# Vision stack of RWKV layers and a graph convolution: loads of x placed in mid-step, the first conv product ahead of the sums, and a variance subtracted by TensorE

## The chip, the cores and the metric

The kernel runs on one core of a Trainium2 chip. The time is that of the device in microseconds (us) for one launch, the median of several runs; less is better. A core has a matrix engine (TensorE, PE), three engines for elementwise work (VectorE or DVE, ScalarE or ACT, GpSimd or POOL), and an engine that only issues transfers (SyncE, SP). Each has its own instruction stream, and semaphores tie the streams together.

## The reference

The input x has 16 images of 192 channels and 56 x 56 pixels in float32. Three layers of one kind follow each other, then one of another kind. Cut to what matters:

```python
for l in 0, 1, 2:
    xs = tokens(group_norm(x, 32 groups))             # [16, 3136, 192]
    k, v, r = xs @ Wk.T, xs @ Wv.T, xs @ Wr.T
    h = sigmoid(r) * 0.5 * (wkv(k, v) + flip(wkv(flip(k), flip(v))))
    h = (h - mean(h)) * rsqrt(var(h) + 1e-5)          # over the 192 channels
    x = x + image((h * ln_g + ln_b) @ Wo.T)
g = group_norm(x)
m = max over the four rolls of g by 2 rows or columns, minus g, and 0
x = x + gelu(batch_norm(conv_1x1(concat(g, m))))
```

`wkv` is a recurrence over the 3136 tokens: a numerator p and a denominator q decay by a factor of each channel at every token and take in exp(k) * v and exp(k); the result is a quotient with a bonus for the present token. The other direction runs the same from the end. The reference carries a running maximum to keep the exponentials in range.

## The kernel before

**Tiles.** The images are taken in pairs. A pair's 192 channels twice are 384 rows, kept as three blocks of 128 partitions: a chunk of 448 tokens (`L`, one seventh of an image, `NL` = 7) is a tile of 128 x 3 x 448. Such tiles live in 33 slots. `Slot(...)` (L502) takes the oldest name of the list `free`, and `give` puts it back at the end; both happen while the program is written, so which tile comes into which slot is fixed by the order of the code, and an instruction that writes into a slot waits for those that still read the tile before. The banks of PSUM are handed out in the same manner (L513 to L523): seven banks, each of which holds 128 x 512.

**Runs and steps.** A pair in a layer is a run. A run of an RWKV layer first goes forward over its seven chunks (units A: products k and v, exp, forward scans, forward quotient), then backward (units B: product r for the gate, backward scans and quotient, mean of both directions, gate, layer norm, output product, new x with its statistics for the next group norm). A run of the conv layer has units C. Two streams of pairs are shifted against each other, so that a step joins a backward chunk of one run with a forward chunk of another. The program has 249 steps. A step can also carry z: statistics of the input of a pair which starts later; for these the chunk of x is loaded for this alone (units Z).

**Order.** Every engine runs in the order in which the code issues its instructions. Each kind of step has an order written by hand, over small functions that issue for one engine each: `both_a` (85 steps, B with A), `both_a_first` (17, B with A where an earlier chunk's layer norm has not begun), `both_c` (42 steps in seven phases of six, B with C), and `forward_a`, `forward_c`, `backward_alone` for the rest. The main loop (L1686 on) passes the units of the present and of the next step (`nback`, `nfront`). In `both_a` the gate product of the next B stands at the start and the keys of the next A in the middle of the step. `of_stage` says which chunk's layer norm stands at which stage; it's spread over two steps or more.

**Transfers of x.** `load_ahead(unit)` (L830) loads the chunk of x for a unit, if it's not there, into a new slot; a unit C also gets a ring of neighbours. All loads and stores of x are issued by SP, in order: before the change the main loop loads the Z chunks of the present step and the backward chunk of two steps ahead, then the step function loads `nback` and `nfront` (mostly only the latter is new), and `store` writes finished output of the conv layer. Later in a step `b_x` stores the new x (L1089).

**Layer norm of a chunk.** `b_squares` (ScalarE) squares the gated h. `b_sums` (L1037 on; TensorE) sums h and its square over channels: rows 0 to 63 (`LO`) of the bank `st` hold the means, 32 equal rows for each image, and rows 64 to 127 (`HI`) the mean squares. `b_rs1` (L1050, ScalarE) squares the mean, `b_rs2` (L1054, VectorE) subtracts it from the mean square, and `b_rs3` (L1059, L1060, ScalarE) takes exp(-0.5 ln(var + eps)). `b_spread` (L1066, TensorE) spreads this over the channels with ones in `pick`; `b_scale` (L1071, VectorE) multiplies, `b_out` does the output product, and `b_x` (L1084, VectorE) adds it to x. The mean itself is taken out by the output weights, which are folded with a centring matrix at the start.

**Other lines that the prediction names.** `scan` (L870): VectorE's scans, three per direction and operand, over 449 elements each. `bonus` (L885): VectorE's `q` or `p` plus bonus. `save` (L881): copies the scan's last state to the next tile. `a_ekv` (L935): exp(k) * v. `a_y` (L977): GpSimd's product of numerator and inverse denominator in the forward direction; it gives back the denominator's slot at once. `b_mix` (L1026 to L1028): GpSimd's three products and sums for the mean of both directions and the gate. `project` (L593 to L602): a product with a folded matrix of 192 x 192 for both images, in float32.

Of the kernel before, what the change touches and what calls it, by code (L numbers as in the profile page):

```python
# [473 lines left out]
def fast_path(ctx: ExitStack, tc: tile.TileContext, flag, x, wproj, wfold, wcfold, wconst, wgroup, sums, picks, vecs, out):  # L474
# [562 lines left out]
    def b_sums(run, c):  # L1037
        h, sq = run.h[c].t, run.ek.pop(c)
        st = run.ps["st"] = bank("st")
        parts = ((h, 0), (h, 1), (sq.t, 0), (sq.t, 1))  # L1040
        for n, (t, i) in enumerate(parts):
            PE.matmul(st[32 * n : 32 * n + 32, :L], ones[:, 0, :], t[:, 2 * i, :], start=True, stop=False)
        for n, (t, i) in enumerate(parts):
            PE.matmul(st[32 * n : 32 * n + 32, :L], ones[:, 1 + i, :], t[:, 1, :], start=False, stop=True)
        sq.give()

    def b_rs1(run, c):
        rs, st = row.tile([P, L], F32, tag="rs", name=name("rs")), run.ps["st"]
        run.rs[c] = rs
        S.activation(rs[HI, :], st[LO, :L], AF.Square)  # L1050

    def b_rs2(run, c):
        rs, st = run.rs[c], run.ps["st"]
        V.tensor_sub(rs[HI, :], st[HI, :L], rs[HI, :])  # L1054
        release(st)

    def b_rs3(run, c):
        rs = run.rs[c]
        S.activation(rs[HI, :], rs[HI, :], AF.Ln, bias=eps4[HI, :])  # L1059
        S.activation(rs[HI, :], rs[HI, :], AF.Exp, scale=-0.5)  # L1060

    def b_spread(run, c):
# [252 lines left out]
        for _ in range(min(most, len(z))):  # L1315
            z_stats(*z.pop(0))

    def both_a(b, a, nback, nfront, z):

        den = lambda: a[0].den[a[1]]  # L1320
        l = of_stage(0.5)
        load_ahead(nback)
        load_ahead(nfront)
        store()
        if nback is not None:
            b_gate(*nback[1:])
            b_exp(*nback[1:])
        count(z)
        b_q(*b)
        if l:  # L1330
            b_rs2(*l)
            b_rs3(*l)
        b_sigmoid(*b)
        a_values(*a)
        if l:
            b_spread(*l)
        b_p(*b)
        b_den(*b)
        for js in (AC, slice(1, 2)):
            ln(b[0].ek[b[1]], js)  # L1340
            exp_minus(b[0].ek[b[1]], js)
        b_num(*b)
        b_mix(*b)
        if l:
            b_scale(*l)
            b_out(*l)
            late[l] = 2
        a_ekv(*a)
        sum_up()
        keys(nfront)  # L1350
        a_q(*a)
        if l:
            add(l)
        b_squares(*b, (0,))
        a_save(*a)
        count(z)
        exp_keys(nfront, (0, 2))
        b_squares(*b, (2,))
        exp_keys(nfront, (1,))
        b_squares(*b, (1,))  # L1360
        b_sums(*b)
        a_p(*a)
        gap()
        a_den(*a)
        b_rs1(*b)
        late[b] = 0.5
        invert(den())
        gap()
        a_num(*a)
        a_y(*a)  # L1370
        gap()

    def both_a_first(b, a, nback, nfront):

        den = lambda: a[0].den[a[1]]
        l = of_stage(0)
        load_ahead(nback)
        load_ahead(nfront)
        store()
        a_values(*a)  # L1380
        b_squares(*l, (0, 2))
# [4 lines left out]
        invert(b[0].ek[b[1]])  # L1386
        b_num(*b)
        b_mix(*b)
        a_ekv(*a)
        b_squares(*l, (1,))  # L1390
        if nback is not None:
# [22 lines left out]
        exp_minus(den())  # L1414
        a_y(*a)

    def both_c(b, a, nback, nfront):

        l0, l1, l2 = of_stage(0), of_stage(1), of_stage(2)
        load_ahead(nback)  # L1420
        load_ahead(nfront)
        store()
        b_q(*b)
        b_p(*b)
        if l0:
            squares_and_sums(l0)
        b_den(*b)
# [7 lines left out]
        if l1:  # L1435
            spread_and_scale(l1)
        gap()
        if nback is not None:
            b_gate(*nback[1:])
            b_exp(*nback[1:])  # L1440
        else:
            keys(nfront)
            exp_keys(nfront)
        c_product(*a, 0)
        c_rows(*a)
        c_columns(*a)
        c_product(*a, 1)
        gap()
        if l0:
            b_rs2(*l0)  # L1450
            b_rs3(*l0)
            late[l0] = 1
        gap()
        b_num(*b)
        b_sigmoid(*b)
# [223 lines left out]
    with tc.manual_schedule(engines={PE.engine, V.engine, S.engine, G.engine, nc.sync.engine}):  # L1679
# [6 lines left out]
        for i, (b, f, z) in enumerate(steps):  # L1686
# [3 lines left out]
            if i == 0:  # L1690
                keys(f)
                exp_keys(f)
            for run, c, _ in z:
                load_ahead(("Z", run, c))
            if i + 2 < len(steps):
                load_ahead(steps[i + 2][0])

            nkeys = nfront if nfront is not None and nfront[0] == "A" else None
            if f and not b and nkeys is None and nfront is not None and i + 2 < len(steps):
# [3 lines left out]
            if f and nback is None and nfront is not None:  # L1703
                near = [u for _, u, _ in steps[i + 1 : i + 4] if u is not None and u[0] == "A"]
                if len(near) > 1 and near[1][1] is near[0][1]:
                    load_ahead(near[1])
            if b and f and f[0] == "A":
                if of_stage(0) is None:
                    both_a(b[1:], f[1:], nback, nfront, z)
                else:  # L1710
                    both_a_first(b[1:], f[1:], nback, nfront)
            elif b and f:
                both_c(b[1:], f[1:], nback, nfront)
            elif f and f[0] == "A":
                forward_a(f[1:], nback, nfront, nkeys, z)
            elif f:
# [60 lines left out]
def _lay_out(inputs):  # L1777
# [10 lines left out]
    for q in layer:  # L1788
# [8 lines left out]
    sums = np.zeros((P, 3, 32), np.float32)  # L1797
    sums[:, 0, :] = sums[0:64, 1, :] = sums[64:P, 2, :] = 1.0 / C

    picks = np.zeros((P, 3, P), np.float32)  # L1800
    picks[64, 0, :] = picks[64, 1, 0:64] = picks[96, 1, 64:P] = picks[96, 2, :] = 1.0
    return {"x": x, "wproj": wproj, "wconv": wconv, "wconst": wconst, "ones": ones, "vecs": vecs,
            "wfold": wfold, "wcfold": wcfold, "wgroup": _pack_rows(group), "sums": sums, "picks": picks}

# [18 lines left out]
```

## Time and profile before

| what | value |
|---|---|
| median of 3 runs | 5291.94 us (5285.85 to 5298.13) |
| the profiled execution's own time | 5294.96 us |
| its span | 5293.2 us |
| mean granted TensorE clock in it | 0.917 of full |
| VectorE busy | 4893.1 us (92%) |
| TensorE busy | 4618.0 us (87%) |
| ScalarE busy | 3705.1 us (70%) |
| GpSimd busy | 2883.5 us (54%) |
| mean HBM traffic | 90 GB/s |
| the subtraction L1054 | 168 times 628 ns, 105.5 us |

The span is the time from the first to the last instruction on the core; busy times are those in which an engine executes. An engine's busy share is an average over steps with different limits, so the waits of each engine and the timeline of single steps have to be read beside it. A row of instructions has its line, engine, operation, output and input with the number of partitions and elements, the count, then the total and mean duration, and the idle time ahead of it with what ended most of it. A row of waits reads: engine, line and tile that waited, what released it, us in total, number of waits, the longest. In a timeline the columns are the start, the duration, and the instruction.

### The profile page before, as it was taken

The page shows a single profiled execution, that of the slowest core. Times are in us where ns is not written, and L with a number is a line of the kernel's source. Part 1 is how long each engine was busy: PE and PEld are TensorE (multiplying, and loading weights), DVE is VectorE, ACT ScalarE, POOL GpSimd, SP SyncE. Part 2 cuts the span into 40 slices and gives each one's busy share as a digit, 9 for nine tenths or more (in the row PEclk, how much of TensorE's full clock was granted, in tenths as well). Part 3 has the DMA queues.
Part 4 walks back from the last instruction along what each step waited for, and adds up shares of the span by engine and source line. Part 5 has one row for each costly group of instructions (what it writes and reads, how often), then busy time and mean ns, then how long its engine had stood idle before and what let it go on. Part 6 is the DMA issues. An engine that isn't in the chain of part 4 may idle for free. (4 is left out here: it accounts for less than half of the span.)

```text
span 5293.2 us, 51222 instructions
## 1 busy us (share of the span) xinstructions
PE 4618.0 (87%) x15206; PEld 1484.1 (28%) x15206; DVE 4893.1 (92%) x6456; ACT 3705.1 (70%) x7163; POOL 2883.5 (54%) x2234
## 2 busy tenths in 40 slices
PE   7888888889798888888979888888897988898897
PEld 3222222223232222222323222222232322222222
DVE  6999899899999998999999999889999999999996
ACT  6777777776666777777666677777756667777672
POOL 1665555554545555555454555555545455566562
PEclk9999989989899899889989988888998999999898
DMA  5222222233332222223333222222333322222233
GB/s 151 68 81 86 83 81 91 84 107 112 92 103 82 74 87 98 71 88 124 93 98 106 74 83 87 86 83 87 122 92 103 92 73 76 78 81 79 69 107 113
DMA packets 314272, 482.43 MB, mean 91 GB/s; under 512 B 66432, under 2 KB 306688, under 8 KB 313984
## 3 DMA queue, kind: packets, MB, share of 16 engines
q1 hardware_dynamic: 312832, 477.59, 28.2%
q8 instruction: 123, 2.02, 0.2%
q10 hardware_dynamic: 1152, 1.48, 0.1%
q14 instruction: 165, 1.35, 0.1%
HBM read 324.83 MB, written 154.14 MB: 90 GB/s over the span
## 5 line engine op out<-in xcount | busy, mean ns | idle before, releaser
L870 DVE TENSOR_TENSOR_SCAN q<-fdecays,ek 128x449 f32<-128x449 f32 (+1 forms) x1008 | 1024.7, 1071 | 60.8 <-POOL p L977 50.5
L870 DVE TENSOR_TENSOR_SCAN p<-fdecays,ekv 128x449 f32<-128x449 f32 (+1 forms) x1008 | 1024.1, 1071 | 44.9 <-POOL p L977 42.4
L977 POOL TENSOR_TENSOR p<-p,q 128x1344 f32<-128x1344 f32 x168 | 512.3, 3050 | 856.6 <-ACT q L973 437.6
L1026 POOL TENSOR_TENSOR ekv<-ekv,ek 128x448 f32<-128x448 f32 x504 | 624.0, 1238 | 588.1 <-ACT ek L973 211.1
L1028 POOL TENSOR_TENSOR p<-p,sg 128x448 f32<-128x448 f32 x504 | 609.3, 1209 | 78.5 <-ACT ek L879 31.9
L1027 POOL TENSOR_TENSOR p<-p,ekv 128x448 f32<-128x448 f32 x504 | 601.7, 1194 | 39.5
L881 POOL COPY ekv<-p 128x3 f32<-128x3 f32 x265 | 231.3, 873 | 678.6 <-DVE p L870 660.0
L915 ACT ACTIVATE ek<-k,k 128x448 f32<-128x448 f32 x504 | 295.2, 632 | 316.0 <-PE k L596 274.8
L593 PE MATMUL ops<-p,fwo 128*128 128x448 f32 x336 | 235.6, 792 | 268.3 <-DVE p L1071 268.1
L1035 ACT ACTIVATE ek<-p 128x448 f32<-128x448 f32 x504 | 282.7, 572 | 217.3 <-POOL p L1028 216.5
L1066 PE MATMUL rsb<-rs,fpicks 32*128 32x448 f32 (+1 forms) x1008 | 353.6, 618 | 90.2 <-ACT rs L1060 90.2
L730 ACT ACTIVATE fjunk<-x 128x448 f32<-128x448 f32 x672 | 387.6, 577 | 41.5 <-DVE x L1084 14.6
L1084 DVE SCALAR_TENSOR_TENSOR x<-ops,fwob,x 128x448 f32<-128x448 f32 x504 | 317.9, 673 | 73.5 <-PE ops L596 39.9
L885 DVE SCALAR_TENSOR_TENSOR ek<-ek,fcc,q 128x896 f32<-128x896 f32 x336 | 374.9, 1156 | 0.1
L729 ACT ACTIVATE fjunk<-x 128x448 f32<-128x448 f32 x600 | 342.5, 571 | 11.4
L885 DVE SCALAR_TENSOR_TENSOR q<-ek,fcc,q 128x896 f32<-128x896 f32 x336 | 345.7, 1070 | 2.2 <-ACT ek L879 1.6
L970 ACT ACTIVATE q<-q 128x1344 f32<-128x1344 f32 x168 | 222.8, 1326 | 162.0 <-DVE q L885 134.0
L991 ACT ACTIVATE sg<-r,r 128x448 f32<-128x448 f32 x504 | 312.9, 627 | 20.1 <-PE r L596 14.4
L935 DVE SCALAR_TENSOR_TENSOR ekv<-v,v,ek 128x448 f32<-128x448 f32 x504 | 313.7, 676 | 12.5 <-PE v L602 7.1
L1071 DVE TENSOR_TENSOR p<-p,rsb 128x448 f32<-128x448 f32 x504 | 281.7, 614 | 46.3 <-PE rsb L1066 46.0
L885 DVE SCALAR_TENSOR_TENSOR ekv<-ekv,fcc,p 128x896 f32<-128x896 f32 x336 | 322.4, 1001 | 1.2
L885 DVE SCALAR_TENSOR_TENSOR p<-ekv,fcc,p 128x896 f32<-128x896 f32 x336 | 294.7, 918 | 4.3 <-POOL ekv L881 2.1
(235 smaller groups left out, 11544.5 us busy)
## 6 DMA issues: line engine op xcount, KB each, us to landing
x<-xd SPq DMA_DIRECT2D x240, 672.0 KB, 5.8
xd<-x SPq DMA_DIRECT2D x168, 672.0 KB, 4.1
x<-in_x_dram SPq DMA_DIRECT2D x320, 224.0 KB, 4.2
x<-in_x_dram SPq DMA_DIRECT2D x320, 112.0 KB, 4.0
out_dram<-ml SPq DMA_DIRECT2D x112, 224.0 KB, 2.3
m<-xd SPq DMA_DIRECT2D x112, 168.0 KB, 5.3
wkv<-in_wfold_dram SPq DMA_DIRECT2D x24, 640.0 KB, 5.3
out_dram<-ml SPq DMA_DIRECT2D x112, 112.0 KB, 2.3
```

The source lines that it names most:

```text
L729: S.activation(junk, xt[:, j, :], AF.Identity, accum_out=stats[:, 0, j, c : c + 1])
L730: S.activation(junk, xt[:, j, :], AF.Square, accum_out=stats[:, 1, j, c : c + 1])
L870: V.tensor_tensor_scan(out, dec[:, column(j)].to_broadcast([P, L if first else L + 1]), e, 0.0, ALU.mult, ALU.add)
L885: by_channel(lambda js, i: V.scalar_tensor_tensor(dst.t[:, js, :], e.t[:, js, :], cc[:, i : i + 1], state.t[:, js, :], ALU.mult, ALU.add))
L935: V.scalar_tensor_tensor(e.t[:, j, :], ps[j][:, 0:L], b[:, j, :], run.ek[c].t[:, j, :], ALU.add, ALU.mult)
L977: G.tensor_mul(run.h[c].t, run.h[c].t, den.t)
L991: S.activation(sg.t[:, j, :], ps[j][:, 0:L], AF.Exp, bias=b[:, j, :], scale=-1.0, accum_out=run.chk[:, at : at + 1])
L1026: G.tensor_mul(y.t[:, j, :], y.t[:, j, :], den.t[:, j, :])
L1027: G.tensor_add(h.t[:, j, :], h.t[:, j, :], y.t[:, j, :])
L1028: G.tensor_mul(h.t[:, j, :], h.t[:, j, :], sg.t[:, j, :])
L1066: PE.matmul(ps[j][:, :L], pick[rows, j, :], rs[rows, :], start=True, stop=True)
L1084: V.scalar_tensor_tensor(xj, ps[j][:, 0:L], wob[:, column(j)], xj, ALU.add, ALU.add, accum_out=run.new[:, 0, j, c : c + 1] if c == 0 else ...
```

## The change

It has three parts. The layer norm's variance: the square of the mean is written to the lower half of its tile, TensorE multiplies it by a negative unit matrix (64 x 64, new in the constant `picks`) and adds it onto the mean square in the bank `st`, and Ln reads the bank. The loads: `nfront`, the Z chunks (now those of the next step) and the backward chunk of two steps ahead go into a list, `loads`, which `both_a` and `both_a_first` load after `b_mix`, and `both_c` after its first `gap` and the conv's `store`; other steps load it at their start, as before. `both_a_first` also takes the slot for the next `ekv` ahead of the loads. The conv step: where no layer norm is at stage 1 and a backward unit follows (`first`), the gate product of the next B, its exp and the first half of the conv product come ahead of the squares and sums. In all of `both_c` the subtraction and what follows it move ahead of `c_columns` and the second conv product.

```diff
--- before.py
+++ after.py
@@ -1041,22 +1041,22 @@
         for n, (t, i) in enumerate(parts):
             PE.matmul(st[32 * n : 32 * n + 32, :L], ones[:, 0, :], t[:, 2 * i, :], start=True, stop=False)
         for n, (t, i) in enumerate(parts):
-            PE.matmul(st[32 * n : 32 * n + 32, :L], ones[:, 1 + i, :], t[:, 1, :], start=False, stop=True)
+            PE.matmul(st[32 * n : 32 * n + 32, :L], ones[:, 1 + i, :], t[:, 1, :], start=False, stop=n < 2)
         sq.give()
 
     def b_rs1(run, c):
         rs, st = row.tile([P, L], F32, tag="rs", name=name("rs")), run.ps["st"]
         run.rs[c] = rs
-        S.activation(rs[HI, :], st[LO, :L], AF.Square)
+        S.activation(rs[LO, :], st[LO, :L], AF.Square)
 
     def b_rs2(run, c):
+        PE.matmul(run.ps["st"][HI, :L], pick[LO, 0, 0:64], run.rs[c][LO, :], start=False, stop=True)
+
+    def b_rs3(run, c):
         rs, st = run.rs[c], run.ps["st"]
-        V.tensor_sub(rs[HI, :], st[HI, :L], rs[HI, :])
+        S.activation(rs[HI, :], st[HI, :L], AF.Ln, bias=eps4[HI, :])
         release(st)
-
-    def b_rs3(run, c):
-        rs = run.rs[c]
-        S.activation(rs[HI, :], rs[HI, :], AF.Ln, bias=eps4[HI, :])
         S.activation(rs[HI, :], rs[HI, :], AF.Exp, scale=-0.5)
 
     def b_spread(run, c):
@@ -1315,12 +1315,11 @@
         for _ in range(min(most, len(z))):
             z_stats(*z.pop(0))
 
-    def both_a(b, a, nback, nfront, z):
+    def both_a(b, a, nback, nfront, z, loads):
 
         den = lambda: a[0].den[a[1]]
         l = of_stage(0.5)
         load_ahead(nback)
-        load_ahead(nfront)
         store()
         if nback is not None:
             b_gate(*nback[1:])
@@ -1341,6 +1340,8 @@
             exp_minus(b[0].ek[b[1]], js)
         b_num(*b)
         b_mix(*b)
+        for u in loads:
+            load_ahead(u)
         if l:
             b_scale(*l)
             b_out(*l)
@@ -1370,12 +1371,11 @@
         a_y(*a)
         gap()
 
-    def both_a_first(b, a, nback, nfront):
+    def both_a_first(b, a, nback, nfront, loads):
 
         den = lambda: a[0].den[a[1]]
         l = of_stage(0)
         load_ahead(nback)
-        load_ahead(nfront)
         store()
         a_values(*a)
         b_squares(*l, (0, 2))
@@ -1386,6 +1386,9 @@
         invert(b[0].ek[b[1]])
         b_num(*b)
         b_mix(*b)
+        slot_of(a[0].ekv, a[1] + 1, "ekv")
+        for u in loads:
+            load_ahead(u)
         a_ekv(*a)
         b_squares(*l, (1,))
         if nback is not None:
@@ -1414,14 +1417,18 @@
         exp_minus(den())
         a_y(*a)
 
-    def both_c(b, a, nback, nfront):
+    def both_c(b, a, nback, nfront, loads):
 
         l0, l1, l2 = of_stage(0), of_stage(1), of_stage(2)
         load_ahead(nback)
-        load_ahead(nfront)
-        store()
+        first = nback is not None and not l1
         b_q(*b)
         b_p(*b)
+        if first:
+            b_gate(*nback[1:])
+            b_exp(*nback[1:])
+            c_product(*a, 0)
         if l0:
             squares_and_sums(l0)
         b_den(*b)
@@ -1435,21 +1442,26 @@
         if l1:
             spread_and_scale(l1)
         gap()
+        store()
+        for u in loads:
+            load_ahead(u)
         if nback is not None:
-            b_gate(*nback[1:])
-            b_exp(*nback[1:])
+            if not first:
+                b_gate(*nback[1:])
+                b_exp(*nback[1:])
         else:
             keys(nfront)
             exp_keys(nfront)
-        c_product(*a, 0)
+        if not first:
+            c_product(*a, 0)
         c_rows(*a)
-        c_columns(*a)
-        c_product(*a, 1)
-        gap()
         if l0:
             b_rs2(*l0)
             b_rs3(*l0)
             late[l0] = 1
+        c_columns(*a)
+        c_product(*a, 1)
+        gap()
         gap()
         b_num(*b)
         b_sigmoid(*b)
@@ -1690,10 +1702,10 @@
             if i == 0:
                 keys(f)
                 exp_keys(f)
-            for run, c, _ in z:
-                load_ahead(("Z", run, c))
-            if i + 2 < len(steps):
-                load_ahead(steps[i + 2][0])
+            ahead = [("Z", run, c) for run, c, _ in (z if not b else [])]
+            ahead += [nfront] if b and f else []
+            ahead += [("Z", run, c) for run, c, _ in (steps[i + 1][2] if i + 1 < len(steps) else [])]
+            ahead += [steps[i + 2][0]] if i + 2 < len(steps) else []
 
             nkeys = nfront if nfront is not None and nfront[0] == "A" else None
             if f and not b and nkeys is None and nfront is not None and i + 2 < len(steps):
@@ -1703,14 +1715,17 @@
             if f and nback is None and nfront is not None:
                 near = [u for _, u, _ in steps[i + 1 : i + 4] if u is not None and u[0] == "A"]
                 if len(near) > 1 and near[1][1] is near[0][1]:
-                    load_ahead(near[1])
+                    ahead.append(near[1])
+            if not (b and f):
+                for u in ahead:
+                    load_ahead(u)
             if b and f and f[0] == "A":
                 if of_stage(0) is None:
-                    both_a(b[1:], f[1:], nback, nfront, z)
+                    both_a(b[1:], f[1:], nback, nfront, z, ahead)
                 else:
-                    both_a_first(b[1:], f[1:], nback, nfront)
+                    both_a_first(b[1:], f[1:], nback, nfront, ahead)
             elif b and f:
-                both_c(b[1:], f[1:], nback, nfront)
+                both_c(b[1:], f[1:], nback, nfront, ahead)
             elif f and f[0] == "A":
                 forward_a(f[1:], nback, nfront, nkeys, z)
             elif f:
@@ -1797,8 +1812,10 @@
     sums = np.zeros((P, 3, 32), np.float32)
     sums[:, 0, :] = sums[0:64, 1, :] = sums[64:P, 2, :] = 1.0 / C
 
     picks = np.zeros((P, 3, P), np.float32)
     picks[64, 0, :] = picks[64, 1, 0:64] = picks[96, 1, 64:P] = picks[96, 2, :] = 1.0
+    picks[0:64, 0, 0:64] = -np.eye(64)
     return {"x": x, "wproj": wproj, "wconv": wconv, "wconst": wconst, "ones": ones, "vecs": vecs,
             "wfold": wfold, "wcfold": wcfold, "wgroup": _pack_rows(group), "sums": sums, "picks": picks}
```

## The prediction

> **What bounds the kernel now.** I read the page's busy times first, then the waits of VectorE and TensorE, then timelines and windows of a steady step of each kind.
>
> ```profile
> span 5293.2 us, 51222 instructions
> PE 4618.0 (87%) x15206; PEld 1484.1 (28%) x15206; DVE 4893.1 (92%) x6456; ACT 3705.1 (70%) x7163; POOL 2883.5 (54%) x2234
> ```
>
> VectorE (DVE) leads at 92%, TensorE (PE) follows at 87%. Only 400.1 us of the span has no VectorE work in it. The timeline of VectorE over one steady `both_a` step, from one subtraction to the next:
>
> ```profile
> 4900.46 0.63 DVE L1054 TENSOR_TENSOR rs<-st,rs 64x448 f32<-64x448 f32 x1
> 4901.12 3.06 DVE L870 TENSOR_TENSOR_SCAN p<-fdecays,ekv 128x449 f32<-128x449 f32 x3
> ...
> 4921.76 3.05 DVE L870 TENSOR_TENSOR_SCAN q<-fdecays,ek 128x449 f32<-128x449 f32 x3
> 4924.83 0.63 DVE L1054 TENSOR_TENSOR rs<-st,rs 64x448 f32<-64x448 f32 x1
> ```
>
> No idle note stands beside any of the rows from 4900 to 4926, and the step lasts 24.37 us (4924.83 - 4900.46). The windows view of the step before it and of this one (columns: length, then busy time of PE, weight loads, DVE, ACT, POOL; then granted PE clock, DMA share, GB/s):
>
> ```profile
> 4876.74:4901.12 24.38, 22.76 (x77) 6.80 (x76) 24.31 (x31) 18.58 (x35) 14.27 (x13) 0.93 0.25 85
> 4901.12:4925.49 24.37, 23.25 (x81) 7.35 (x82) 24.31 (x30) 20.20 (x40) 16.05 (x13) 1.00 0.17 58
> ```
>
> VectorE is full to 0.06 us; TensorE has 1.1 to 1.6 us to spare. Where VectorE isn't full, its list of waits says for what:
>
> ```profile
> DVE q L870 <- POOL p L977: 50.5, 9, 6.1
> DVE p L1071 <- PE rsb L1066: 46.0, 28, 4.8
> DVE p L870 <- POOL p L977: 42.4, 21, 2.6
> DVE ekv L881 <- POOL p L1027: 24.6, 9, 2.8
> ```
>
> A scan (L870) that waits for GpSimd's product in `a_y` (L977) doesn't need its data. It writes into a slot that `a_y` still reads (the denominator): its tile is the next in the free list. That comes where loads of x for the next statistics took the older free slots at the start of the step. The two rows make 92.9 us in 30 waits.
>
> **What the Trainium skill says.** "FP8 and Floating Point Precision", section TensorE Precision Notes: true FP32 takes four passes through the array. The trace agrees in cost: full-width fp32 products of 448 columns start 0.95 us apart. "TensorE: Matmul & The Clock Gate", Part 1: a monitor halves TensorE's clock when it has been idle over windows of about 3.4 us. Here the clock is 0.57 of full in 4884 to 4888 after a wait of 1.62 us; in the trace partial idleness is enough, so the page's "idle" must be read loosely. The same page, Architectural detail: TensorE pulls weight loads ahead, while ScalarE and VectorE are strictly first in, first out; so what stands behind a waiting Square or product waits too. It's why the place of the new product counts.
>
> **The subtraction, in `both_a` (85 steps).** The row by form:
>
> ```profile
> L1054 DVE TENSOR_TENSOR rs<-st,rs 64x448 f32<-64x448 f32 x168 | 105.5, 628 | 24.3 <-ACT rs L1050 19.1
> L1059 ACT ACTIVATE rs<-rs,feps 64x448 f32<-64x448 f32 x168 | 111.4, 663 | 60.3 <-DVE rs L1054 57.8
> L1066 PE MATMUL rsb<-rs,fpicks 64*128 64x448 f32 x336 | 186.8, 639 | 0.0
> ```
>
> VectorE loses 0.63 us, and the two scans beside it can overlap by 0.08 again instead of standing 0.03 apart: 0.7 us a step. TensorE gains one fp32 product of 64 rows, two instructions; the trace has none of 64 by 64. Nearest are L1066 of 64 rows (0.639 per instruction, pipelined) and a full-width product, 0.95 us apart. The bounds are 0.5 (as cheap as one pipelined instruction) and 1.3 (two of 0.639, with nothing overlapped); I take 0.95, since rows of 64 and of 128 take about the same per instruction (0.639 and 0.631). TensorE's share of a step rises from 22.1 us at full clock (23.25 modelled ends, less overlaps) to 23.05, against 24.37 - 0.7 = 23.65 for VectorE. It still fits, and the extra product sits in a hole where TensorE would wait for `b_scale` (the output product L593 waits for L1071: 268.1 us in 128 waits). The chain Square, product, Ln, Exp, spread, scale isn't longer than before, since the product at 0.95 takes the place of 0.63 on a full VectorE. In `both_a` its Square was issued near the end of the step before, so the product waits for nothing, and the bank of the sums is held only until Ln instead of until the subtraction, some 0.6 us longer, with seven banks in turn. A half-clock window costs about 1.7 us (half of 3.4), but a fuller TensorE should have fewer of them. Unhidden coupling takes a part: I count 0.5 of the 0.7. 85 x -0.5 = -42 us (0 to -62). The 17 chunks whose subtraction stands in `forward_a`: -0.7 each, -12.
>
> **The loads in mid-step.** Moved past `load_ahead` at the start are x for the next forward unit, the next step's Z chunks (one step earlier in the program), and x of the backward unit two steps on; one DMA each of 672 KB, 5.8 us from issue to landing, on SP's queue, and now behind `store`. SP is mostly held by the store of new x (L1089 on L1084: 2803.4 us), so in time they leave when that is done, if their slot is free. At the start of a step with Z the free list holds five or six slots; now `sg`, `q` and `p` take the first ones and the scans' wait on L977 goes: -92.9 us at most. What is late next: `a_p`'s output is popped later and gets the slot which GpSimd's `b_mix` still reads, in about 21 steps at up to 1.7 us: +35. Net -58 (-93 to -30). The transfers wait for younger slots on SP, out of any engine's way; x for `keys` (needed some 15 us into the step) lands by about 12. If that cover is gone, a late chunk costs its excess, up to 5.8 us, in each such step.
>
> **`both_a_first` (17 steps).** Here all of the chain is in one step: sums, Square, product, Ln, Exp, spread, scale. The product is queued on TensorE ahead of `keys`, so keys wait for the Square (0.54 us) and product (0.95): about +1.6 us at the scale, where slack is nil, in 8 steps: +13. In the 9 with Z the new early slot for `ekv` ends the L881 wait of 2.7 us: -0.6 each net. Sum +7 (-10 to +25).
>
> **`both_c` (42 steps, seven phases of six).** In the first step of a phase TensorE stands for GpSimd's gate products ahead of the sums; timeline of TensorE:
>
> ```profile
> 1105.73 1.70 PE L1042 MATMUL st<-p,fsums 128*32 128x448 f32 x2 [7.40 <-POOL p L1028]
> 1111.01 0.96 PE L1042 MATMUL st<-p,fsums 128*32 128x448 f32 x1 [3.58 <-POOL p L1028]
> ...
> 1114.93 0.96 PE L1044 MATMUL st<-p,fsums 128*32 128x448 f32 x2 [1.61 <-POOL p L1028]
> ```
>
> That is 12.6 us of waiting, and the r product and the first half of the conv product (about 4.5 us each, fourteen instructions) fit into it. After it VectorE waits:
>
> ```profile
> 1132.91 1.69 DVE L1071 TENSOR_TENSOR p<-p,rsb 128x448 f32<-128x448 f32 x3 [4.22 <-PE rsb L1066]
> ```
>
> With 9 us of products done earlier this wait goes, and a little more: -5 x 7 = -35 (-15 to -50). In the next four steps of a phase (28) the products also come first, and now sums wait behind them. A loop forms: r 4.51 + conv half 4.51 + sums 2.0, Square 0.54, ScalarE's exp 1.33 and statistics 4.07, Ln and Exp 1.27, spread to scale 1.06, 0.65 to the output product, 4.51: 24.5 us, against 23.8 to 25.6 in four steps before. No gain, and it is an idle stretch for TensorE's clock: +0.7 each, +20 (-10 to +60). The sixth step, without early products, pays the 0.95: +6. `forward_c`: -5.
>
> **Sum.** -42 - 12 - 58 + 7 - 35 + 20 + 6 - 5 = -119 us against the profiled execution's own 5294.96 (span 5293.2 and 1.8 around it): 5176. That execution was 3.0 above the median of 5291.94, so the median should be about 5174.
>
> **Rivals.**
> A, a smaller gain. TensorE follows VectorE so closely that the freed 0.7 us returns as waits on L1071 or `ops`, and slot waits come back at other tiles. Both_a 0, forward -12, slots -25, `both_a_first` +7, first conv steps -25, others +25: -30, about 5262. For it: 128 waits of TensorE on the scale, and a free list that only moves the wait. Against: a VectorE without a gap.
> B, slower. TensorE becomes the bound in `both_a` at its mean granted clock: 23.05 / 0.917 = 25.1 us, 0.77 over the present 24.37, 85 x 0.77 = +65; `both_a_first` +27, `both_c` +25 in all, slots -58: +59, about 5351. It decides from the point at which the wait between spread and scale reaches zero on TensorE's side while half-clock windows persist. For it: clock 0.917. Against: those windows follow idle TensorE, and the step of 4901 ran at clock 1.00.
> C, a larger gain. The full 0.7 in every step (-60), slot waits gone with nothing behind (-93), first conv steps -45, others 0, forward -17, `both_a_first` 0: -215, with a better clock; I put it at about 5080.
>
> **How the numbers follow.** Forecast 0.52, A 0.22, B 0.14, C 0.12. My own case reaches from about 5110 to 5240; the range takes in A and stops short of C and B, at 5105 to 5285. Less than 0.2% (10.6 us) can't be told from no change: of A a fifth falls there or above. Faster 0.80, same 0.05, slower 0.15.
>
> **What would show it.** L1054 as a DVE row is gone and a PE row of 64 by 64 has 336 instructions of 0.5 to 0.65 us. The steady step falls from 24.37 to about 23.9; VectorE still without gaps there. Waits on L977 fall from 92.9 to under 20, and waits on L1028 or on the gate appear at `a_p`. The 4.2 us at the scale of each conv phase's first step is gone. TensorE's clock is at or above 0.917. Wrong would be: a wait of several us of VectorE on L1066 in each `both_a` step (B), or waits of `keys` on a DMA (loads too late).

## The result, and the profile after

The changed kernel takes 5243.42 us (median of 4 runs, 5241.4 to 5246.37) against 5295.03 us for the kernel before measured beside it: ratio 0.9905, with a 95% interval of 0.9888 to 0.9922. That is 52 us less, about 1% of the time; the forecast had 121 us.

The page of the changed kernel, span and busy times:

```profile
span 5244.4 us, 51899 instructions
...
PE 4701.2 (90%) x15542; PEld 1493.0 (28%) x15542; DVE 4837.0 (92%) x6288; ACT 3680.4 (70%) x7163; POOL 2900.0 (55%) x2234
```

VectorE's busy time fell by 56.1 us only (4893.1 to 4837.0), though the 168 subtractions of 105.5 us left it: other VectorE work has become longer. Most of that is in the conv layer's products. The one that grew most, before and then in the changed kernel:

```profile
L1120 DVE TENSOR_TENSOR ml<-x 128x416 f32<-128x416 f32 x168 | 98.8, 588 | 9.1 <-POOL p L1028 8.9
```

```profile
L1120 DVE TENSOR_TENSOR ml<-x 128x416 f32<-128x416 f32 x168 | 153.6, 914 | 8.9 <-POOL p L1028 8.9
```

TensorE's busy time rose by 83 us, and its mean granted clock from 0.917 to 0.943. The new product's rows by form, and what stands around it:

```profile
L1054 PE MATMUL st<-rs,fpicks 64*64 64x448 f32 x336 | 168.9, 584 | 41.8 <-ACT rs L1050 41.8
...
L1058 ACT ACTIVATE rs<-st,feps 64x448 f32<-64x448 f32 x168 | 105.8, 629 | 42.0 <-PE st L1054 37.4
```

The product costs 0.58 us an instruction; its two instructions together take 0.96 us in the timelines. The list of VectorE's waits, to be put beside that of before (us in total, times, longest):

```profile
DVE p L1071 <- PE rsb L1066: 92.0, 54, 18.6
DVE p L870 <- POOL p L1027: 60.1, 18, 6.8
DVE p L870 <- POOL p L1028: 53.6, 6, 9.0
...
DVE gt L772 <- ACT rstd L753: 20.3, 8, 3.3
```

The waits for `a_y` (L977) and the one at L881, 92.9 and 24.6 us before, are gone. In their place the numerator's forward scan waits for `b_mix` (L1027, L1028) for 113.7 us. So 117.5 us of slot waits became 113.7. The first row, the wait for the scale's input, stood at 46.0 us before.

Where the time went can be read step by step. I took the start of GpSimd's first product in each `b_mix` as a mark, which gives 168 marks in either trace, and summed the differences by kind of phase (a phase is the seven backward chunks of one run, with the forward-only steps after it). In us against the kernel before:

| phase | change, us |
|---|---|
| five with A, no Z: `both_a_first` | +8.1 |
| the same: 20 middle steps | -17.2 |
| the same: last step and forward steps | -3.9 |
| twelve with A and Z: `both_a_first` | +25.0 |
| the same: 48 middle steps | -42.4 |
| the same: last step and forward steps | -19.6 |
| seven with C: first step | -25.3 |
| the same: the three steps after it | +60.0 |
| the same: the rest | -30.9 |
| start and end | -2.6 |

By phase: A without Z -13.0, A with Z -37.0, conv +3.8. The same marks sort the waits for the scale's input: they are gone in the first conv steps (28.7 us before), but rose from 3.4 to 33.7 us in `both_a_first` and from 12.3 to 41.0 in the last and forward-only steps of the conv phases (18.6 of it is one wait near the program's end, which stood at the subtraction before, with 16.1 us).

A middle step without Z, in the changed kernel (timeline of VectorE and the windows view of the step before, whose columns are length; busy PE, weight loads, DVE, ACT, POOL; clock, DMA share, GB/s):

```profile
4876.83 3.05 DVE L870 TENSOR_TENSOR_SCAN q<-fdecays,ek 128x449 f32<-128x449 f32 x3
4879.80 3.03 DVE L870 TENSOR_TENSOR_SCAN p<-fdecays,ekv 128x449 f32<-128x449 f32 x3
4882.75 1.72 DVE L885 SCALAR_TENSOR_TENSOR ek<-ek,fcc,q 128x896 f32<-128x896 f32 x2
4884.39 1.74 DVE L885 SCALAR_TENSOR_TENSOR ekv<-ekv,fcc,p 128x896 f32<-128x896 f32 x2
4886.05 1.67 DVE L1071 TENSOR_TENSOR p<-p,rsb 128x448 f32<-128x448 f32 x3
```

```profile
4839.20:4862.76 23.56, 23.25 (x82) 7.11 (x80) 23.56 (x30) 19.24 (x38) 15.23 (x13) 1.00 0.26 88
```

The scans of q and p follow each other with no subtraction between. VectorE is busy for the whole step, and the scale at L1071 waits for nothing. These 20 steps went from 24.33 us on average to 23.47.

### The profile page after: what moved, and what is told of

It is laid out like the page before. It is cut to its first block, busy times and chain, and to the rows that moved or that the text cites. A ratio compares the mean times of both kernels' runs of the same rounds, so it can differ in the third digit from the quotient of the medians.

```text
span 5244.4 us, 51899 instructions
## 1 busy us (share of the span) xinstructions
PE 4701.2 (90%) x15542; PEld 1493.0 (28%) x15542; DVE 4837.0 (92%) x6288; ACT 3680.4 (70%) x7163; POOL 2900.0 (55%) x2234
## 3 DMA queue, kind: packets, MB, share of 16 engines
q8 instruction: 125, 2.05, 0.2%
## 5 line engine op out<-in xcount | busy, mean ns | idle before, releaser
L977 POOL TENSOR_TENSOR p<-p,q 128x1344 f32<-128x1344 f32 x168 | 511.6, 3045 | 838.2 <-ACT q L973 543.0
L1028 POOL TENSOR_TENSOR p<-p,sg 128x448 f32<-128x448 f32 x504 | 633.3, 1257 | 144.5 <-ACT ek L879 101.3
L1027 POOL TENSOR_TENSOR p<-p,ekv 128x448 f32<-128x448 f32 x504 | 600.9, 1192 | 39.5
L881 POOL COPY ekv<-p 128x3 f32<-128x3 f32 x265 | 221.8, 837 | 538.5 <-DVE p L870 531.5
L1066 PE MATMUL rsb<-rs,fpicks 32*128 32x448 f32 (+1 forms) x1008 | 342.0, 602 | 46.8 <-ACT rs L1060 46.8
L991 ACT ACTIVATE sg<-r,r 128x448 f32<-128x448 f32 x504 | 313.1, 627 | 95.6 <-PE r L596 72.3
L1071 DVE TENSOR_TENSOR p<-p,rsb 128x448 f32<-128x448 f32 x504 | 281.7, 615 | 92.0 <-PE rsb L1066 92.0
L1050 ACT ACTIVATE rs<-st 64x448 f32<-64x448 f32 x168 | 90.2, 537 | 358.0 <-PE st L1044 358.0
L593 PE MATMUL ops<-p,fwo 128*128 128x448 f32 x336 | 210.0, 713 | 139.6 <-DVE p L1071 139.3
```

The costliest lines, as they stand in the source:

```text
L977: G.tensor_mul(run.h[c].t, run.h[c].t, den.t)
L1027: G.tensor_add(h.t[:, j, :], h.t[:, j, :], y.t[:, j, :])
L1028: G.tensor_mul(h.t[:, j, :], h.t[:, j, :], sg.t[:, j, :])
L1066: PE.matmul(ps[j][:, :L], pick[rows, j, :], rs[rows, :], start=True, stop=True)
L1071: V.tensor_mul(h[:, j, :], h[:, j, :], ps[j][:, :L])
```

## The experiments

Each kernel was timed in five rounds beside the kernel before, whose median lay between 5290 and 5295 us, so differences between kernels of different tables are good to some 5 us. Line numbers are those of each kernel's own source: a helper may stand some lines lower than in the kernel before. Sums by phase come from the profiled execution of each.

### One part at a time

Three kernels carry one part each. The edits are the parts of the diff shown above: `e1` the product with the negative unit matrix (with its move ahead of `c_columns`), `e2` the loads, `e3` the order in `both_c`.

> Only the variance's subtraction goes to TensorE (its place in both_c included); loads and the conv order as before. Theory M (the layer norm's edit is what paid; loads only moved the slot waits; the conv order lost in its later steps): steady both_a steps without Z fall from 24.37 to about 23.6 us, 85 x -0.8 = -68, forward_a 17 x -0.7 = -12, both_a_first 17 x +1.6 = +27, together about -50 us (-65 to -35). Rival R (TensorE takes the freed time back and the loads paid): -10 us (-25 to +5), with waits on L1066 in both_a. The forecast on record had -42 - 12 + 13 + some for this part.

> Only the loads go to mid-step (with the early slot for ekv and the later store in both_c); subtraction on VectorE, conv order as before. Theory M: VectorE's waits for a slot stay at about 115 us in sum, but under L1027 and L1028 in place of L977 and L881; the time is -5 us (-20 to +15). Rival R: waits for slots fall under 40 us and the time by 45 us or more; then their return in the changed kernel would be due to the other two parts.

> Only the order in both_c: gate product, its exp and the first conv half ahead of squares and sums; subtraction on VectorE, loads at the start. Theory M: first step of each of seven phases -3.5 us (-25 in sum), the third-to-last step of six phases +5 to +6 (a next run's group norm begins there), other later steps +1 to +2: together +15 us (0 to +35), slower than before. Rival R: -25 us, the later steps lose only through the subtraction's product or the loads.

| kernel | median us | ratio (95% interval) | A, no Z | A with Z | conv |
|---|---|---|---|---|---|
| e1, subtraction alone | 5328.15 | 1.0062 (1.0049 to 1.0076) | -12.5 | -53.4 | +98.8 |
| e2, loads alone | 5270.84 | 0.9954 (0.994 to 0.9967) | +3.3 | -25.0 | -0.5 |
| e3, conv order alone | 5370.70 | 1.0146 (1.013 to 1.0162) | +3.5 | -14.9 | +81.4 |
| all three | 5243.42 | 0.9905 (0.9888 to 0.9922) | -13.0 | -37.0 | +3.8 |

My theory had the loads at -5 and got -24.5; it had the subtraction at -50 and the conv order at +15, and both are slower by far more than either theory allowed. The phases show how. In the phases with A the subtraction alone gives the whole gain, 66 us. The loads alone give 22 us there, and the three parts don't add up: -88, and -11 that come with the conv order (it shifts which slot comes to whom, presumably the cause), would be -99, and together they give -50. In the conv phases two edits that cost 99 and 81 us alone cost 4 us together.

In `e1` the dearest of the conv steps is the one in which the next run's group norm is worked out. Timelines of ScalarE, of TensorE and of VectorE:

```profile
1212.76 0.54 ACT L1050 ACTIVATE rs<-st 64x448 f32<-64x448 f32 x1 [0.22 <-PE st L1044]
...
1226.84 0.63 ACT L1058 ACTIVATE rs<-st,feps 64x448 f32<-64x448 f32 x1 [4.67 <-PE st L1054]
...
1228.10 0.20 ACT L752 ACTIVATE rstd<-var 128x3 f32<-128x3 f32 x1
```

```profile
1215.19 1.86 PE L593 MATMUL r<-x,wr 128*128 128x448 f32 x2
...
1225.84 0.96 PE L1054 MATMUL st<-rs,fpicks 64*64 64x448 f32 x2
```

```profile
1228.57 0.16 DVE L772 TENSOR_TENSOR gt<-rstd 128x3 f32<-128x3 f32 x1 [8.07 <-ACT rstd L753]
```

The Square is ready at 1213.3, but on TensorE the group norm's small products, the r product and the first conv half stand ahead of the new product. It starts at 1225.84, so Ln comes at 1226.84; ScalarE stands for 4.67 us, the group norm's rstd is queued behind Ln, and VectorE stands 8.07 us for it.

### A slot kept for the scan

```diff
         slot_of(a[0].ekv, a[1] + 1, "ekv")
+        kept["p"] = Slot("p")          # taken by scan() in a_p
         for u in loads:
```

> The changed kernel with one line more: in both_a_first the slot of a_p's output is taken ahead of the mid-step loads, so that it isn't the gate's or the backward numerator's slot that b_mix still reads. Theory M: the nine waits of 6.8 to 9.0 us (74 us) on L1027 and L1028 go and the time falls to about 5175 us, 65 to 75 us under the changed kernel. If the wait only moves to the next allocation of VectorE or ScalarE in the step: 0 to -20 us against the changed kernel. If the waits did not lie on the path: no change.

5230.71 us (ratio 0.9878, 0.986 to 0.9896): 13 us under the changed kernel, not 70. VectorE's waits:

```profile
DVE q L872 <- POOL p L1029: 59.6, 6, 11.0
DVE p L872 <- POOL p L1029: 39.4, 15, 2.9
```

The six long waits have gone on to the other forward scan, which now gets the slot that `b_mix` reads. The free list is short; a slot that is taken early for one tile makes the next one take a young slot.

### No scan on a slot that b_mix reads

```diff
# both_a and both_a_first
-        for u in loads:
-            load_ahead(u)
+        for u in loads:
+            if u is None or u[0] != "Z":
+                load_ahead(u)
...
         a_p(*a)
+        for u in loads:
+            load_ahead(u)
```

(with the kept slot of the run before in `both_a_first`)

> The changed kernel with slots given out in another order: Z loads after a_p in both_a and both_a_first, and the slot of a_p's output taken ahead of the loads in both_a_first, so that no forward scan writes into a slot that b_mix of the same step reads. Theory M (the freed slots are the limit, and the waits lie on the path): VectorE's waits on GpSimd's b_mix fall from 114 to under 20 us and the time by 80 to 100 us, to about 5155. Rival S (GpSimd's chain itself limits these steps and the waits only show it): the waits go, but waits on the scale or on ops come in their place, and the time falls by at most 30 us.

5227.75 us (0.9881, 0.9865 to 0.9896): 16 us less than the changed kernel, as rival S had it. No wait of a scan on `b_mix` is left in the list, and this leads it:

```profile
DVE p L1073 <- PE rsb L1068: 183.1, 81, 18.6
```

In `both_a_first` with Z the 53 us came (+25.0 became -28.0 against before). There the waits had been time. In the middle steps with Z 37 us were lost again (-42.4 became -5.5), though VectorE no longer waits for a slot there. So the waits for slots in the middle steps were not what set their length. What sets it can be followed in the changed kernel's timelines, of GpSimd and then of ScalarE, over one step with Z:

```profile
782.72 1.15 POOL L1026 TENSOR_TENSOR ekv<-ekv,ek 128x448 f32<-128x448 f32 x1 [5.79 <-ACT ek L973]
...
792.26 1.13 POOL L1028 TENSOR_TENSOR p<-p,sg 128x448 f32<-128x448 f32 x1
...
808.71 1.14 POOL L1026 TENSOR_TENSOR ekv<-ekv,ek 128x448 f32<-128x448 f32 x1 [3.13 <-ACT ek L973]
```

```profile
799.54 0.61 ACT L991 ACTIVATE sg<-r,r 128x448 f32<-128x448 f32 x1
...
801.37 0.57 ACT L729 ACTIVATE fjunk<-x 128x448 f32<-128x448 f32 x1
...
802.86 0.63 ACT L1058 ACTIVATE rs<-st,feps 64x448 f32<-64x448 f32 x1
...
804.12 1.33 ACT L998 ACTIVATE sg<-sg 128x1344 f32<-128x1344 f32 x1
...
806.71 0.94 ACT L970 ACTIVATE ek<-ek 128x896 f32<-128x896 f32 x1
807.68 0.95 ACT L973 ACTIVATE ek<-ek 128x896 f32<-128x896 f32 x1
```

It is a loop of 26.0 us (782.72 to 808.71): the mix (`b_mix`) to 793.4, squares and sums, the r product, the gate's exp at 799.54, a statistic of z at 801.37, the layer norm's Ln and Exp, the sigmoid, Ln and Exp of the backward ek, and the next mix. VectorE's wait in the same step lies beside the loop:

```profile
792.21 3.06 DVE L870 TENSOR_TENSOR_SCAN p<-fdecays,ekv 128x449 f32<-128x449 f32 x3 [2.93 <-POOL p L1027]
795.19 1.72 DVE L885 SCALAR_TENSOR_TENSOR q<-ek,fcc,q 128x896 f32<-128x896 f32 x2
```

Take it away and VectorE arrives earlier at the scale and waits there. The step even grew, from 26.0 to 27.3 us. In `e5` (VectorE, then GpSimd), with no wait, VectorE's bonus product and GpSimd's last mix product fall together and both take longer, 2.60 for 1.72 us and 2.05 for 1.13:

```profile
784.63 2.60 DVE L887 SCALAR_TENSOR_TENSOR q<-ek,fcc,q 128x896 f32<-128x896 f32 x2
```

```profile
784.70 2.05 POOL L1030 TENSOR_TENSOR p<-p,sg 128x448 f32<-128x448 f32 x1
```

The Trainium skill ("SBUF — State Buffer", section SBUF: two separate sides) has the mechanism: a port pair that VectorE's operations with two SBUF inputs and GpSimd share is held by one of them for a whole instruction. The pairs of durations agree. The mix as a whole takes 11.56 us in place of 10.67, which is 0.9 of the 1.3 us. The other 0.4 lies between the mix and the gate's last exp, where TensorE had a lower clock. Windows of the changed kernel, then of `e5` (the clock is the third number from the end):

```profile
793.39:800.80 7.41, 7.36 (x25) 2.25 (x26) 7.41 (x9) 4.93 (x9) 1.99 (x2) 1.00 0.28 95
```

```profile
786.75:794.60 7.85, 7.80 (x23) 2.42 (x24) 7.77 (x9) 5.04 (x9) 3.02 (x2) 0.78 0.59 176
```

This is the account of one step; the 48 middle steps with Z lost 0.77 us each on average.

### The subtraction back on VectorE in both_a_first

```diff
-        b_sums(*l)        # the variance on TensorE
-        b_rs1(*l)
+        b_sums(*l, 4)     # as in the kernel before
+        v_rs1(*l)
```

(and the same for the two steps after it)

> The changed kernel with VectorE's subtraction back in both_a_first alone (17 steps), where the whole layer norm is in one step. Theory M (the product adds about 1.6 us to that step's chain through TensorE): 17 x -1.6 = -27 us against the changed kernel, about 5216. Rival (the step's length is set by the slot waits, the chain hides behind them): 0 to -10 us, since only the eight steps without Z gain.

5241.79 us (0.9911, 0.9897 to 0.9924): no gain to speak of, 1.6 us. `both_a_first` itself fell by 20 us in sum, but the conv phases rose by 10 us and the other steps of the phases with A by 6. The chain through TensorE costs time in these steps (in the five phases without Z +8.1 became 0.0), but what the edit frees was taken up elsewhere. Why the conv phases, which this edit doesn't touch, should take some of it stays open.

### Which conv steps gain from the early products

```diff
-        first = nback is not None and not l1
+        first = nback is not None and b[1] == NL - 2
```

> The changed kernel with the early gate and conv products in the first step of each conv phase only; subtraction on TensorE everywhere. Theory M (with sums ahead of r and the first conv half, the product for the subtraction stands 9 us behind the Square, and Ln blocks what is behind it on ScalarE): later conv steps lose as in the kernel with the subtraction alone, +50 to +90 us against the changed kernel. Rival T (in the later steps early products cost, because sums wait behind them): -30 to -50 us.

In the second kernel `both_c` has in addition the subtraction on VectorE, at its place of before.

> As the run before, and in both_c the subtraction back on VectorE at its old place. Theory M: the later conv steps are as in the kernel before and the first ones keep their gain of 25 us; the conv phases go from +4 to about -28 us against the kernel before, so about -30 us against the changed kernel (5213). If the first step's gain needs the product too (the order alone gave only -4.5 there): 0 to -8 us against the changed kernel.

`e7` takes 5292.43 us (1.0002, 0.9994 to 1.001), 49 us more than the changed kernel: with sums ahead of r again, the product on TensorE holds the later steps up as in `e1` (conv phases +57.2). `e8` takes 5184.47 us (0.9802, 0.9788 to 0.9816), 59 us less than the changed kernel and twice what I had expected. Its conv phases stand at -49.7: -25.3 in the first step, as in the changed kernel, -6.0 in the three after it in place of +60.0, and -18.0 in the last and forward steps. `e8` changes two things in the later steps at once; `e3` has the early products there with the subtraction on VectorE, and its three steps after the first stand at +85.8 (the loads alone, `e2`, leave them at +0.4). So the early products pay in the first of the six steps. In the later ones they push the sums back by two products, some 9 us, and cost time where the subtraction is VectorE's; where it is TensorE's, at its place behind the conv half, they cost less than their absence (+60.0 in the changed kernel, +95.3 in `e7`).

### The product right behind the Square

The kernel `e1` with two moves in `both_c`: the product goes right behind the Square, and Ln and Exp go back to the subtraction's place in the kernel before.

```diff
         if l0:
             b_rs1(*l0)
+            b_rs2(*l0)
         exp_minus(b[0].ek[b[1]])
...
         c_rows(*a)
-        if l0:
-            b_rs2(*l0)
-            b_rs3(*l0)
-            late[l0] = 1
         c_columns(*a)
         c_product(*a, 1)
         gap()
+        if l0:
+            b_rs3(*l0)
+            late[l0] = 1
```

> The kernel with the subtraction alone on TensorE, loads and conv order as before, but in both_c the product stands right behind the Square, ahead of r and of both conv halves, and Ln at its old place. Theory M (the 99 us that this kernel lost in the conv phases come from r and the first conv half, 9 us, standing between the Square and the product, and from ScalarE held up behind Ln): conv phases about as before, so some 85 to 100 us less than with the subtraction alone, 5230 to 5245. If the product's own 0.95 us, or Ln's reading of the bank, is what costs: 5300 or more.

5219.91 us (0.9874, 0.9854 to 0.9894), 108 us less than `e1`, and conv phases at -3.7 in place of +98.8. Product and Ln are the same instructions as in `e1`; their places alone made the loss. Timeline of TensorE, then of ScalarE, where the group norm's rstd now goes ahead of Ln:

```profile
1203.71 0.96 PE L1054 MATMUL st<-rs,fpicks 64*64 64x448 f32 x2 [0.66 <-ACT rs L1050]
...
1206.03 1.02 PE L593 MATMUL r<-x,wr 128*128 128x448 f32 x2
```

```profile
1211.67 0.20 ACT L752 ACTIVATE rstd<-var 128x3 f32<-128x3 f32 x1 [0.30 <-DVE var L750]
...
1212.14 0.63 ACT L1058 ACTIVATE rs<-st,feps 64x448 f32<-64x448 f32 x1
```

TensorE stands 0.66 us for the Square. How much of the 108 us the product's place gave and how much Ln's wasn't separated. The place isn't free in every step either: the first steps of the conv phases stand at +20.0 us (+22.8 in `e1`), with VectorE waiting 55.0 us for the scale's input there (28.7 before), and the other conv steps at -23.7. This kernel, with the subtraction as its only edit, took 24 us less than the whole change (ratios 0.9874 against 0.9905).

### What follows from them together

`e9` joins `e8` with the slot order of `e5` in `both_a_first` alone. `e10` is `e9` with one line of `both_a` moved, and `e11` is `e10` with the subtraction of `both_a_first` on VectorE.

```diff
# e10, both_a
-        count(z)
         b_q(*b)
...
             exp_minus(b[0].ek[b[1]], js)
+        count(z)
         b_num(*b)
```

> The kernel of the last run (early conv products in each phase's first step only, subtraction on VectorE in both_c) with the slot order of the slots run in both_a_first alone; both_a keeps its loads in mid-step. If conv phases and the phases with Z are independent, the first steps with Z give the 53 us that they gave in the slots run and the middle ones lose nothing: 5184 - 53 = 5131. If the freed time only goes on to the middle steps as in the slots run: about 5170.

> As the run before, and in both_a the first of a step's two statistics of z is issued on ScalarE after Ln and Exp of the backward ek, in place of right after the gate's exp. Theory L (with Z the middle steps are set by a loop GpSimd's mix, sums, r product, gate's exp, one statistic of 1.3 us, Ln and Exp, sigmoid, ek's Ln and Exp, mix; VectorE's slot wait lies beside it): the statistic leaves the loop, 36 to 48 steps by 1.0 to 1.3 us, -35 to -60 us against the run before, though neither VectorE's nor TensorE's work changes. If slot waits or VectorE set these steps: 0 to -10 us.

> As the run before, and in both_a_first the subtraction back on VectorE. Now that no slot wait stands in these steps: if TensorE's chain sets them, 17 x -1.6 = -27 us against the run before; if what the chain frees is taken elsewhere, as in the first try of this edit (-1.6 us in all), 0 to -8 us.

| kernel | median us | ratio (95% interval) | A, no Z | A with Z | conv |
|---|---|---|---|---|---|
| e9 | 5132.27 | 0.971 (0.969 to 0.973) | -15.9 | -95.6 | -51.4 |
| e10 | 5086.97 | 0.962 (0.96 to 0.9639) | -16.0 | -139.4 | -49.0 |
| e11 | 5073.66 | 0.9595 (0.9575 to 0.9614) | -16.4 | -152.3 | -53.4 |

`e9` came out at 5132 where 5131 stood: the gains of the conv phases and of the phases with Z add up. `e10` took a statistic of 1.3 us out of the loop read above and gained 45 us; no engine's work changed, and the 48 middle steps with Z fell from 24.83 to 23.97 us on average. That shows that the loop, and not VectorE or the slots, sets these steps. The slot waits that are left shrank by themselves, without a change to the slots of the scans that made them, from 39.5 us in `e9` to this:

```profile
DVE p L872 <- POOL p L1029: 21.5, 15, 1.6
```

`e11` gained 13 us more, half of the 27 that its chain's arithmetic gave. It is 3.1% faster than the changed kernel (0.9595 over 0.9905) and the best that was run.

## Why the prediction was off

**The step that failed is the one on slots**, a wait that was priced as time: "now `sg`, `q` and `p` take the first ones and the scans' wait on L977 goes: -92.9 us at most [...] Net -58". Two things were wrong in it. The wait didn't go, it changed its name: 117.5 us for L977 and L881 before, 113.7 for L1027 and L1028 after. I had seen that `a_p`'s output would get a slot which `b_mix` reads, but took 35 us for it, from 1.7 us in 21 steps; in `both_a_first`, where the loads take three old slots at once, it's 6.8 to 9.0 us in nine steps. There I had booked a gain of 2.7 us each for L881. And the row of waits wasn't a row of time: `e5` took all of it away and gained 16 us. In `both_a_first` the waits were time (53 us came back), but in the middle steps with Z VectorE's waits lie beside a loop over GpSimd, TensorE and ScalarE. I had taken VectorE for the bound in all A steps from timelines of steps without Z. The loads alone are worth 24 us, where -58 stood.

**The subtraction in `both_a`** was right in its mechanism and too small: 0.5 of 0.7 us was counted for each of 85 steps. The middle steps without Z gained 0.86 us each on average, in the change and in `e1` alike, so at least the whole 0.7 came. TensorE didn't take it back; rival B was wrong, and the clock rose, as I had expected of a fuller TensorE. The subtraction alone gave 66 us in the phases with A, where the terms -42, -12 and +7 make -47.

**The two gains don't add.** Loads and subtraction alone give 22 and 66 us in the phases with A; the change got 50. The subtraction makes VectorE faster and the loop of the Z steps no shorter, so that part of what it frees only lengthens the wait for `b_mix`: with the loads alone L1027 and L1028 hold VectorE for 93 us, with the subtraction as well for 114. That is 21 of the 38 us that are missing; the rest isn't explained.

**`both_a_first`**: +1.6 us for the chain through TensorE was right in size where no Z is (+8.1 in five phases). The waits for the scale's input, 30 us more than before, fit this chain. The term as a whole, +7, measured +33, and without the nine slot waits (`e5`) -20. (Its net of -0.6 in a step with Z was a slip: +1.6 and -2.7 make -1.1.)

**The conv phases** were forecast at -14 with `forward_c` and measured +4. The first step's -35 was -25.3 in the interval that follows it, and its wait on L1066 is gone. The later steps, +20 with a range to +60, are at +60.0 in the three after the first. The arithmetic of their loop left two things out. One is the step with the next run's group norm, where the rstd is late behind statistics and Ln; that step has +37.5 of the +60.0, and VectorE stands for rstd for 20.3 us in eight waits. The other is VectorE's products in `c_rows` and `c_columns`, which now fall together with GpSimd's later work:

```profile
1210.83 3.45 DVE L1120 TENSOR_TENSOR ml<-x 128x416 f32<-128x416 f32 x1
...
1214.38 0.58 DVE L1120 TENSOR_TENSOR ml<-x 128x416 f32<-128x416 f32 x1
```

It's the same operation twice, 3.45 us while GpSimd multiplies 128x1344 elements (3.08 us) and 0.58 after it. The row L1120 is long in the kernels that lose in the later conv steps (161.2 us in `e1`, 153.7 in `e3`) and short in those that don't (101.8 in `e8`, 100.5 in `e12`). But it isn't the loss itself: in `e6` it fell to 136.5 while the conv phases rose, and in the step shown ScalarE is busy up to rstd without it, while TensorE's second conv half waits 1.13 us for it. How much each of the two takes wasn't separated. What experiments show is that the early products in the later steps lose by themselves (`e3` against `e8`), and that they are needed there only because the subtraction's product would otherwise stand behind 9 us of products (`e7`, `e12`).

Of the cases, A (a smaller gain, slot waits that come back at other tiles) names what happened to the slots, at 5262 against 5243. That its sum lies so near is in part luck: it put `both_a` at 0, where the subtraction paid, and `both_a_first` at +7. Its part on the slots should have been the likeliest: the working of the forecast itself had a free list from which another tile would take the young slot. And the signs that the forecast named came true (the steady step, the waits on L977, those in the first conv steps, the clock) though its sum did not: none of them priced the slots.

## What to carry to other kernels

A wait for a buffer is not time until the loop that sets the step has been followed through all engines in a step of the very kind in which the wait stands; ask of each waiting engine what it would wait for next. Where buffers come from a list in the order of the code, taking one earlier only hands the young one to the next taker: count who takes what, step kind by step kind, before pricing it. A small product that is moved onto a TensorE that takes products in order costs its place, not its 0.96 us: behind 9 us of other products, with Ln waiting ahead of other work, it cost 99 us in the conv phases; right behind its input, with Ln later, it cost 20 us in the first steps and nothing in the sum.

## What the runs showed of the hardware that I hadn't expected

An fp32 product of 64 by 64 with 448 columns took as long per instruction (584 ns) as one with 128 rows and columns (591 ns for r in the kernel before): fewer rows saved nothing. The forecast had taken this from products of 64 rows by 128; for 64 by 64 it was new. The granted clock doesn't follow the time: it was 0.930 in `e1` (5328 us) and 0.937 in `e7` (5292 us), against 0.917 in the kernel before (5295 us), 0.943 in the changed one and 0.952 in `e11` (5074 us). How much of a gain is the clock's was not tried. And a VectorE operation of 0.58 us was stretched to 3.45 us beside a GpSimd product of 3.08 us, which makes the moment at which GpSimd works a cost of VectorE's.
